# Half of one more part of a mixing stage moved between the experts, with its sums kept in DRAM

## The chip, the cores and the metric

The kernel runs on one core of a Trainium2 chip. The metric is the device time of one execution in microseconds (us). Engines are named as the profile names them: PE (matrix multiplication; PEld is its weight load), DVE (elementwise work, scans and reductions), ACT (activation functions), POOL (elementwise work, no access to PSUM), SP (issues the DMAs).

## The reference, cut to what matters

Two layers run over x of 16 batches, 256 tokens and 128 features, all in float32. Layer 0 is attention with 16 heads, then a mixture of 16 experts. Layer 1 is a "holographic" attention, then a token mixing block. The change concerns the passage from the experts to the holographic attention, whose core is (H = 16 heads of 64, so 1024 columns; T = 256):

```python
h = _layernorm(x) * (1 + ca) + sa
k = exp(1j * (h @ Wk) * 10)            # a phase for each token and column
v = h @ Wv
rotors = exp(1j * t * freqs)           # the same for all batches
out_pos   = real(cumsum(v * rotors)          * conj(rotors)) / sqrt(t + 1)
out_assoc = real(cumsum(v * conj(shifted k)) * k)            / sqrt(t + 1)
out = (out_pos * gate[:, 0] + out_assoc * gate[:, 1]) @ Wo
x = x + ga * out
```

The real part of a product of complex numbers is two real sums (cosine and sine), so each column needs four running sums over time: two for `pos` (the rotor's half) and two for `assoc`.

## The kernel before

Two batches make a chunk: eight chunks of 512 tokens (`NCH`). The 1024 columns of the holographic attention are eight parts of 128 (`NJ`), numbered 0 to 7. The kernel has three stages.

**Attention of layer 0** (0 to 304 us). The change doesn't touch it.

**Experts** (304 to 672 us). A loop over 128 steps, step n being expert e = n mod 16 of chunk c = n div 16. `gate_up(n)` multiplies the gate and the up weights into PSUM (pg, three banks, line 764; pup, two banks, line 766); DVE makes g (line 768), ACT u (770) and the Silu (773), POOL clamps u (774). One step later `act(n-1)` lets DVE make the product (780) and POOL weigh it by the score (781); three steps later `down(n-3)` adds it into the chunk's accumulator (789). The score rows come as `wide` loads on SP, four steps ahead. All the compute engines run in the order in which the program issues their instructions.

Between the steps stands other work, each piece at a fixed e, or a generator that advances once a step:
- e = 2 to 4: the end of the chunk before (`chunk_end1`, `with_tokens`, `into_stream`). e = 5: DVE takes mean and variance of its rows (`figures`, lines 182 and 183). e = 7: POOL makes the factors (`normalizer`, lines 188 to 193). These are "the stream's figures".
- `prepare` (as `ready`) makes rotors, scaled weights and, in `first_steps`, the first two parts of the late stage. `past_others` keeps its matmuls out of steps in which others use the one spare PSUM bank `p_m`.
- `last_end` finishes the last chunk's attention and its routing (steps 1 to some 34).
- `part_ahead(c)` (line 885) starts at e = 8 of the next chunk, for the six chunks below `AHEAD`. It computes part 7 of chunk c in full, in eight pieces (pos or assoc, batch k, cosine or sine s) of 256 elements: POOL multiplies (`bind`, 903), a step later DVE scans (909) and multiplies by gate and probe (911), a step later DVE adds (916). A piece takes two steps. The sum stays in SBUF in `totals[c]`.

**Holographic attention and mixing** (673 to 1060 us, then an end of 20). A loop over 58 steps (c, j): 7 parts in each of the first six chunks, 8 in the last two. In step n PE projects keys and values of step n+2 (pk 1135, pv 1139), ACT rounds (`whole`, 1136) and copies v; DVE scans `assoc` (1172, into `m_assoc`), scans `pos` (into the PSUM tile `mem`), takes the phase of step n+2 (`phases`, off, 1151) and multiplies mem by the rotor (m_pos, 1408); POOL multiplies m_assoc of step n-1 by its phasor (1413) and binds both halves of step n+1 (1169); ACT makes the sines of step n+2 (1157 to 1159); PE multiplies m_assoc of n-1, later m_pos of n, into the chunk's output `pos[c]` (1186, two matmuls each). At j = 3 one matmul adds `totals[c]` with `w_last` (1195). At j = 0 ACT reads the output of the chunk before (`gated_out`, 1204). The mixing block of the chunks before is spread over the same steps by `place`; its figures come from running sums on ACT (`mix_means`, `mix_figures`, lines 1242 and 1251) and two operations on POOL (`mix_spread`, 1266).

At the end the last two batches run as two generators, advanced together by `both_halves`, beside the last outputs of the chunk before (`mix_out`).

Of the kernel before, what the change touches and what calls it, by code (L numbers as in the profile page):

```python
# [41 lines left out]
AHEAD = NCH - 2  # L42
PARTS = [NJ - 1 if c < AHEAD else NJ for c in range(NCH)]
# [11 lines left out]
def tile_adaln_two_layers(ctx: ExitStack, tc: tile.TileContext, a: dict, out: bass.AP):  # L55
# [130 lines left out]
    def normalizer(c, mv, pool, tag):  # L186
# [7 lines left out]
        return rstd, off  # L194

# [31 lines left out]
    with ExitStack() as moe_scope:  # L227
# [500 lines left out]

        late = ctx.enter_context(tc.tile_pool(name="late", bufs=1, side="right"))
# [11 lines left out]
        w_last = load_late("w_last", [P, D], a["Wo"][HD - P :, :])  # L741
        w_assoc = load_late("w_assoc", [P, NJ, D], a["Wo"].rearrange("(j p) f -> p j f", p=P))
        with ExitStack() as scope:
# [141 lines left out]
            def part_ahead(c):  # L885
# [9 lines left out]
                v = cross.tile([P, 2, T], F32, tag="o", name=f"v_ahead_{c}")  # L895
                pv = p_m.tile([P, 2, T], F32, tag="m", name=f"pv0_{c}")
                nc.tensor.matmul(pv, w_v1[:, ts(j, P)], flat, start=True, stop=True)
                nc.scalar.copy(v, pv)
                bound = {}

                def bind(nm, k, s, by):
                    t = cross.tile([P, T], F32, tag=("heads", "y")[s], name=f"bound_ahead_{nm}_{c}_{k}_{s}")
                    nc.gpsimd.tensor_tensor(t, v[:, k, :], by, ALU.mult)
                    bound[nm, k, s] = t

                written = set()

                def read(nm, k, s, i, probe):
                    nc.vector.tensor_tensor_scan(row, keep_all, bound.pop((nm, k, s)), 0.0, ALU.mult, ALU.add)
                    dst = row if k in written else totals[c][:, k, :]  # L910
                    nc.vector.scalar_tensor_tensor(dst, row, gates[:, j, i : i + 1], probe, ALU.mult, ALU.mult)

                def added(k):
                    if k in written:
                        dst = totals[c][:, k, :]
                        nc.vector.tensor_tensor(dst, row, dst, ALU.add)
                    written.add(k)
# [3 lines left out]
                pos_ = [("pos", k, s, 0, rotor[:, j, s, :], rotor[:, j, s, :]) for k in range(2) for s in range(2)]  # L921
                assoc_ = [("assoc", k, s, 1, cs[:, s, k, 0:T], cs[:, s, k, 1:]) for k in range(2) for s in range(2)]
# [7 lines left out]
                pieces = assoc_ + pos_  # L930
# [6 lines left out]
                for i in range(9):  # L937
                    if i:
                        yield
                        q = pieces[i - 1]  # L940
                        read(*q[:4], q[5])
                    if i < 8:
                        q = pieces[i]
                        bind(*q[:3], q[4])
                    yield
                    if i:
                        added(pieces[i - 1][1])

            def past_others(steps=1):

                while any((at["step"] + i) % NE in (3, 7, *range(10, 16)) for i in range(steps)):
                    yield

            def first_steps():

                flat = hTs[0].rearrange("p k t -> p (k t)")
                for n in range(2):
# [68 lines left out]
            totals = [late.tile([P, 2, T], F32, tag=f"total{c}", name=f"total{c}") for c in range(AHEAD)]  # L1026
# [34 lines left out]
            for n in range(total + 4):  # L1061
# [21 lines left out]
                if e == 5 and c:  # L1083
                    mv = figures(c - 1, "a1")
                if e == 7 and c:
                    figs[c - 1] = normalizer(c - 1, mv, fp, "a1")
# [9 lines left out]
                if e == 8 and 1 <= c <= AHEAD:  # L1096
                    ahead.append(part_ahead(c - 1))
# [6 lines left out]
    with ExitStack() as scope:  # L1104
# [16 lines left out]
        another(hp1)  # L1121
# [38 lines left out]

        def rot(n):
            return rotor[:, steps[n][1], :, :].unsqueeze(2).to_broadcast(both)

        def binders(n):
            w = work[n]
            v2 = w["v"].unsqueeze(1).to_broadcast(both)
            for nm, bind in (("pos", rot(n)), ("assoc", phasor[n % 3][:, :, :, 0:T])):
# [3 lines left out]
        def summed(n, nm, dst):  # L1171
            nc.vector.tensor_tensor_scan(  # L1172
                dst.rearrange("p s k t -> p (s k t)"),
                keep.rearrange("p s t -> p (s t)"),
                work[n][nm].rearrange("p s k t -> p (s k t)"),
# [5 lines left out]
        def out_project(n, i, w, m):  # L1181
# [11 lines left out]
            if i == 0 and j == 3 and c < AHEAD:  # L1193

                nc.tensor.matmul(
                    pos[c], w_last, totals[c].rearrange("p k t -> p (k t)"), start=False, stop=False
                )
# [30 lines left out]
        mix = {}  # L1228

# [7 lines left out]

        def mix_means(c, pool=hp):
            total, less = (pool.tile([P, 4], F32, tag=f"{nm}_f1", name=f"{nm}_f1_{c}") for nm in ("total", "less"))
            unused = hp.tile([P, D], F32, tag="unused", name=f"unused_{c}", bufs=1)  # L1240
            for i in range(4):
                nc.scalar.activation(unused, x[2 * c + i // 2][:, i % 2, :], AF.Copy, accum_out=total[:, i : i + 1])
            nc.scalar.activation(less, total, AF.Copy, scale=-1.0 / D)
            mix[c] = unused, less

        def mix_figures(c, pool=hp):

            unused, less = mix[c]
# [130 lines left out]
        for n in range(last + 2):  # L1379
# [18 lines left out]
            if n <= last:  # L1398
# [4 lines left out]
                if n:  # L1403
                    summed(n, "assoc", m_assoc)
# [194 lines left out]
```

## Time and profile before

| | us |
|---|---|
| time before, median of 3 runs | 1081.39 (1079.85 to 1081.78) |
| the profiled execution's own time | 1081.84 |
| its span, first to last instruction | 1080.1 |
| first gate matmul of the experts | 303.4 |
| first scan of the late stage | 673.4 |
| a gate matmul to the next, in most expert steps | 2.57 |
| the same for 16 steps (64 to 80) | 45.5 |
| m_pos to m_pos, parts 3 to 6 of chunks 2 to 5 | 6.43 |
| seven late steps, chunks 2 to 4 | 46.9 |

Mean times of single operations, from the groups of instructions (line, shape, ns):

| operation | ns |
|---|---|
| DVE scan, 128x1024 (1172) | 2282 and 2274 |
| DVE scan, 128x256 (909) | 691 |
| DVE product m_pos, 128x1024 (1408) | 1215 |
| DVE product, gate and probe, 128x256 (911) | 484 to 493 |
| DVE add, 128x256 (916) | 418 |
| POOL product, 128x1024 (1169, 1413) | 2182 |
| POOL product, 128x256 (903) | 704 |
| POOL clamp and product, 128x512 (774, 781) | 634, 1281 |
| ACT sum of a row, 128x128 (1242) and its read | 306, 186 |
| ACT squares of a row, 128x128 (1251) and its read | 398, 187 |

How to read the profile: busy time of an engine is the sum of its records, which overlap a little at their ends; a float32 matmul is two MATMUL records. In the timeline a line has start, length, engine, source line, operation, output and inputs; in brackets stands the idle time of the engine before it and who ended it. In windows the columns are the busy times of PE, PEld, DVE, ACT and POOL, then the granted PE clock as a share of full speed, and the DMA's share.

### The profile page before, as it was taken

What the parts mean: (1) busy time and instruction counts of PE and PEld (TensorE: products, weight loads), DVE (VectorE), ACT (ScalarE), POOL (GpSimd) and SP (SyncE); (2) the same over time, 40 slices, a digit from 0 to 9 for tenths busy, and PEclk for the clock granted to TensorE, in tenths of its full rate; (3) what the DMA queues carried; (4) which work ended last, traced back from release to release, by engine and by line L of the source; (5) the groups of instructions that cost most, each with busy time, mean ns of one, the idle gap of its engine ahead of it and who ended that gap; (6) DMA issues with size and microseconds to landing.
All of it is one profiled execution on the core that took longest, in us unless ns stands there. A gap on an engine that the chain in (4) does not pass through costs nothing.

```text
span 1080.1 us, 16033 instructions
## 1 busy us (share of the span) xinstructions
PE 1023.5 (95%) x5333; PEld 519.6 (48%) x5333; DVE 909.9 (84%) x1409; ACT 682.3 (63%) x1383; POOL 803.1 (74%) x750
## 2 busy tenths in 40 slices
PE   7999999999999999999999999889999999999987
PEld 5566666666654444444444444333444343434434
DVE  6678878998756789887777778999999999999995
ACT  3676677667656566676766554556676666767662
POOL 2245434533557678888877888999999999999992
PEclk8999999999999999999999999999999999999999
DMA  4102100000052222222222221000000000000000
GB/s 116 42 11 61 53 13 3 2 4 2 4 175 95 82 99 85 93 99 99 95 82 88 89 98 59 1 0 0 1 5 6 10 1 10 1 10 5 5 11 20
DMA packets 31955, 46.80 MB, mean 43 GB/s; under 512 B 8032, under 2 KB 22784, under 8 KB 31872
## 3 DMA queue, kind: packets, MB, share of 16 engines
q1 hardware_dynamic: 31328, 45.51, 12.8%
q8 instruction: 42, 0.69, 0.3%
q14 instruction: 41, 0.34, 0.1%
q10 hardware_dynamic: 544, 0.26, 0.1%
HBM read 43.13 MB, written 2.37 MB: 42 GB/s over the span
## 4 chain that ended last, share of the span: by engine, by line
PE 59%; DVE 23%; ACT 6%; POOL 6%; issue 4%; DMA 1%; SPq 0%; DVEq 0%; ACTq 0%; POOLq 0%
PE pg L764 9%; PE acc L789 9%; PE pup L766 9%; DVE sum_assoc L1172 7%; DVE mem L1172 6%; PE s L404 5%; PE st L438 5%; PE po L458 5%; DVE m_pos L1408 4%; PE pout L1186 3%; PE pq L531 2%; DVE maxima L416 1%; POOL bound_pos L1169 1%; POOL u L781 1%; PE pk L539 1%
## 5 line engine op out<-in xcount | busy, mean ns | idle before, releaser
L446 ACT ACTIVATE exp<-st 128x512 f32<-128x512 f32 x256 | 132.2, 602 | 87.0 <-PE st L438 87.0
L416 DVE TENSOR_REDUCE maxima<-s 128x2 f32<-128x512 f32 x256 | 159.0, 685 | 26.5 <-PE s L404 26.3
L781 POOL TENSOR_TENSOR u<-u,wide 128x512 f32<-128x512 f32 x128 | 163.9, 1281 | 16.1 <-DVE u L780 6.3
L770 ACT ACTIVATE u<-pup,b_gu 128x512 f32<-128x512 f32 x128 | 87.6, 684 | 108.9 <-PE pup L766 100.9
L1186 PE MATMUL pout<-m_pos,w_pos 128*128 128x512 f32 x228 | 114.7, 627 | 32.1 <-DVE m_pos L1408 23.2
L768 DVE TENSOR_SCALAR g<-pg,b_gu 128x512 f32<-128x512 f32 x128 | 95.6, 747 | 58.2 <-PE pg L764 56.9
L789 PE MATMUL acc<-u,w_dn 128*128 128x512 f32 x256 | 132.3, 599 | 3.0 <-POOL u L781 2.8
L1172 DVE TENSOR_TENSOR_SCAN sum_assoc<-keep,bound_assoc 128x1024 f32<-128x1024 bf16 x58 | 132.3, 2282 | 1.8 <-POOL bound_assoc L1169 1.7
L1172 DVE TENSOR_TENSOR_SCAN mem<-keep,bound_pos 128x1024 f32<-128x1024 bf16 x58 | 131.9, 2274 | 0.0
L764 PE MATMUL pg<-hT,w_gu 128*128 128x512 f32 x256 | 131.5, 595 | 0.4 <-DVE logits L638 0.4
L766 PE MATMUL pup<-hT,w_gu 128*128 128x512 f32 x256 | 130.7, 592 | 0.0
L1169 POOL TENSOR_TENSOR bound_assoc<-v,phasor 128x1024 f32<-128x1024 f32 x57 | 124.3, 2181 | 3.9 <-ACT phasor L1159 3.9
L1413 POOL TENSOR_TENSOR sum_assoc<-sum_assoc,phasor 128x1024 f32<-128x1024 f32 x58 | 126.6, 2183 | 0.4 <-DVE sum_assoc L1172 0.4
L1169 POOL TENSOR_TENSOR bound_pos<-v,rotor 128x1024 f32<-128x1024 f32 x57 | 124.4, 2182 | 0.0
L774 POOL TENSOR_SCALAR u<-u 128x512 f32<-128x512 f32 x128 | 81.1, 634 | 56.6 <-ACT u L770 49.8
L1186 PE MATMUL pout<-sum_assoc,w_assoc 128*128 128x512 f32 x228 | 107.5, 594 | 1.2 <-POOL sum_assoc L1413 1.2
L780 DVE SCALAR_TENSOR_TENSOR u<-u,pg 128x512 f32<-128x512 f32 x128 | 87.0, 679 | 15.7 <-POOL u L774 14.4
L1186 PEld LDWEIGHTS pout<-m_pos,w_pos 128*128 128x128 f32 x228 | 40.4, 192 | 102.0 <-DVE m_pos L1408 53.5
L773 ACT ACTIVATE pg<-g 128x512 f32<-128x512 f32 x128 | 76.1, 594 | 16.8 <-DVE g L768 16.7
L1136 ACT ACTIVATE whole<-pk 128x512 f32<-128x512 f32 x56 | 33.4, 596 | 84.2 <-PE pk L1135 84.0
L438 PE MATMUL st<-qx,kx 32*128 32x256 f32 x1024 | 82.4, 390 | 0.9 <-DMA qx<-turned 0.8
L404 PE MATMUL s<-kx,qx 32*128 32x256 f32 x1024 | 78.1, 409 | 4.2 <-DVE kx L541 1.8
(305 smaller groups left out, 1835.1 us busy)
## 6 DMA issues: line engine op xcount, KB each, us to landing
wide<-scores SPq DMA_DIRECT2D x64, 512.0 KB
qx<-turned SPq DMA_DIRECT2D x256, 1.0 KB
w_gu<-in_gate_up_dram SPq DMA_DIRECT2D x8, 256.0 KB
out_dram<-x SPq DMA_DIRECT2D x16, 128.0 KB
x<-in_x_dram SPq DMA_DIRECT2D x14, 128.0 KB
w_dn<-in_down_dram SPq DMA_DIRECT2D x4, 256.0 KB
ga<-ga_rows SPq DMA_DIRECT2D x1, 768.0 KB
w_k<-in_Wk_dram SPq DMA_DIRECT2D x1, 512.0 KB
```

The costliest lines, as they stand in the source:

```text
L404: nc.tensor.matmul(s[g][:, i, :], qs[c][r][rows_, k, ts(i, P)], ks[c][rows_, r // NS, k, :], start=True, stop=True,)
L416: nc.vector.tensor_reduce(mx[:, :, g], s[g], AX.X, ALU.max, negate=True)
L438: nc.tensor.matmul(st[g][:, i, :], ks[c][rows_, r // NS, k, ts(i, P)], qs[c][r][rows_, k, :], start=True, stop=True,)
L446: nc.scalar.activation(e[:, g, :, :], st[g], AF.Exp, scale=QSCALE)
L764: nc.tensor.matmul(pg, w_gu[:, e, 0 : 2 * D : 2], h2, start=True, stop=True)
L766: nc.tensor.matmul(pu, w_gu[:, e, 1 : 2 * D : 2], h2, start=True, stop=True)
L781: nc.gpsimd.tensor_tensor(u, u, wide[n // SOME][:, n % SOME, :], ALU.mult)
L789: nc.tensor.matmul(accs[c], w_dn[:, e, :], work.pop(n), start=False, stop=(e == NE - 1))
L1169: nc.gpsimd.tensor_tensor(w[nm], v2, bind, ALU.mult)
L1172: nc.vector.tensor_tensor_scan(dst.rearrange("p s k t -> p (s k t)"), keep.rearrange("p s t -> p (s t)"), work[n][nm].rearrange("p s k t - ...
L1186: nc.tensor.matmul(pos[c], w[:, j, :], m[:, k, :, :].rearrange("p k t -> p (k t)"), start=(j == 0 and i == 0 and k == 0), stop=(c < NCH - ...
L1413: nc.gpsimd.tensor_tensor(m, m, phasor[(n - 1) % 3][:, :, :, 1:], ALU.mult)
```

## The change

- Among the experts, `part_ahead` becomes `parts_ahead`: it also computes the `pos` half of part 6, so there are twelve pieces instead of eight and one more values matmul for each of the six chunks (at e = 0). A piece is bound in steps with e mod 4 not 0, and read, product and add included, in the step after it. The twelve pieces end at e = 0, sixteen steps after the first.
- The sums of parts 6 and 7 are stored to DRAM (two DMAs of 256 KB for each chunk, on SP) and fetched in the late stage at j = 1 (`fetched`), to be multiplied at j = 6 and j = 3 (`with_fetched`). `w_last` holds two parts' weights.
- In the late stage, a step of part 6 in the first six chunks is a half step (`is_half`): no binding, scan or products of `pos`; the scan of `assoc` is cut in two (cosine into `mem`, sine into `m_assoc`); DVE multiplies the cosine half, POOL only the sine half; one matmul with the fetched sum stands where two with m_pos stood.
- The stream's figures among the experts (e = 5, 6, 7) are made by `mix_means`, `mix_figures` and `mix_spread` instead of `figures` and `normalizer`.
- All three phasor tiles are made in `first_steps`, and its matmuls keep out of e = 0 as well.
- At the end one `both_halves` goes ahead of the two `mix_out`.

```diff
-            def part_ahead(c):
+            def parts_ahead(c):
...
+                def read(q, nm, k, s, i, probe):
+                    nc.vector.tensor_tensor_scan(row, keep_all, bound.pop((q, nm, k, s)), 0.0, ALU.mult, ALU.add)
+                    dst = sum_of[q][:, k, :]
+                    more = (q, k) in written
+                    gate = gates[:, q, i : i + 1]
+                    nc.vector.scalar_tensor_tensor(row if more else dst, row, gate, probe, ALU.mult, ALU.mult)
+                    if more:
                         nc.vector.tensor_tensor(dst, row, dst, ALU.add)
...
+                yield
+                yield
+
+                vs[j - 1] = values(j - 1)
+                pieces = assoc + pos_ + pos_before
+                late_one = None
+                for step in range(1, NE + 1):
+                    yield
+                    if late_one:
+                        read(*late_one[:5], late_one[6])
+                        late_one = None
+                    if step % 4 and pieces:
+                        late_one = pieces.pop(0)
+                        bind(*late_one[:4], late_one[5])
+                for q in (j, j - 1):
+                    nc.sync.dma_start(totals[c, q], sum_of[q])
...
-                while any((at["step"] + i) % NE in (3, 7, *range(10, 16)) for i in range(steps)):
+                while any((at["step"] + i) % NE in (0, 3, 7, *range(10, 16)) for i in range(steps)):
...
                 if e == 5 and c:
-                    mv = figures(c - 1, "a1")
+                    mix_means(c - 1, fp, behind)
+                if e == 6 and c:
+                    mix_figures(c - 1, fp)
                 if e == 7 and c:
-                    figs[c - 1] = normalizer(c - 1, mv, fp, "a1")
+                    mix_spread(c - 1, fp)
+                    figs[c - 1] = mix.pop(c - 1)
...
-            for nm, bind in (("pos", rot(n)), ("assoc", phasor[n % 3][:, :, :, 0:T])):
+            for nm, bind in (("pos", rot(n)), ("assoc", phasor[n % 3][:, :, :, 0:T]))[is_half(n) :]:
...
+        def fetched(c):
+
+            for q in (NJ - 1, NJ - 2):
+                t = hp.tile([P, 2, T], F32, tag=f"there{q}", name=f"fetched_{c}_{q}", bufs=1)
+                nc.sync.dma_start(t, totals[c, q])
+                pos[c, q] = t
...
+                if half:
+
+                    summed(n, "assoc", mem, slice(0, 1))
+                    summed(n, "assoc", m_assoc, slice(1, 2))
+                elif n:
                     summed(n, "assoc", m_assoc)
-                summed(n, "pos", mem)
+                if not half:
+                    summed(n, "pos", mem)
                 if n and n + 2 <= last:
                     phases(n + 2)
-                nc.vector.tensor_tensor(m_pos, mem, rot(n), ALU.mult)
+                if half:
+                    nc.vector.tensor_tensor(m_assoc[:, 0], mem[:, 0], phasor[n % 3][:, 0, :, 1:], ALU.mult)
+                else:
+                    nc.vector.tensor_tensor(m_pos, mem, rot(n), ALU.mult)
...
-                nc.gpsimd.tensor_tensor(m, m, phasor[(n - 1) % 3][:, :, :, 1:], ALU.mult)
+                part = slice(1 if is_half(n - 1) else 0, 2)
+                nc.gpsimd.tensor_tensor(m[:, part], m[:, part], phasor[(n - 1) % 3][:, part, :, 1:], ALU.mult)
...
-                out_project(n, 0, w_pos, m_pos)
+                if is_half(n):
+                    with_fetched(c, j, w_last[:, 0])
+                else:
+                    out_project(n, 0, w_pos, m_pos)
+                if j == 1 and c < AHEAD:
+                    fetched(c)
+                if j == 3 and c < AHEAD:
+                    with_fetched(c, NJ - 1, w_last[:, 1])
...
         both_halves()
+        both_halves()
         for k in range(2):
             mix_out(2 * gone + k, py[:, k])
-        both_halves()
         both_halves()
```

## The prediction

> **What bounds the kernel now.** I read the page first, then the windows by stage, then the timeline of two places that the change touches.
>
> ```profile
> PE 1023.5 (95%) x5333; PEld 519.6 (48%) x5333; DVE 909.9 (84%) x1409; ACT 682.3 (63%) x1383; POOL 803.1 (74%) x750
> ...
> PE 59%; DVE 23%; ACT 6%; POOL 6%; issue 4%; DMA 1%; SPq 0%; DVEq 0%; ACTq 0%; POOLq 0%
> ```
>
> The averages mix two stages with different bounds, which the windows separate (columns: length, then PE, PEld, DVE, ACT and POOL busy).
>
> ```profile
> 487.00:533.00 46.00, 46.00 (x116) 20.90 (x116) 35.26 (x67) 33.85 (x70) 37.88 (x48) 1.00 0.26 93
> ...
> 880.00:930.00 50.00, 46.93 (x117) 20.40 (x116) 48.45 (x39) 35.76 (x76) 48.94 (x25) 1.00 0.02 6
> ```
>
> The reader is to see where the busy time reaches the window's length: among the experts (304 to 672) PE does, in the late stage (673 to 1060) DVE and POOL are at 97%. Costs on the path are counted from start to start in the timeline, since records overlap: a matmul of 512 columns is two PE records of 0.59 that start 0.43 apart, 0.86 in all, and an expert step of three takes 2.57; a late step takes 6.43. So the change carries work from a stage bound by DVE to one bound by PE. All times below are us.
>
> **The half step.** Part six in a chunk of the before, c=2 (step n=20), and the next scan:
>
> ```profile
> 805.51 1.21 DVE L1408 TENSOR_TENSOR m_pos<-mem,rotor 128x1024 f32<-128x1024 f32 x1
> ...
> 806.64 0.41 DVE L1303 TENSOR_TENSOR x<-py,x 128x256 f32<-128x256 f32 x1
> ...
> 806.77 1.99 PE L1186 MATMUL pout<-m_pos,w_pos 128*128 128x512 f32 x4 [0.57 <-DVE m_pos L1408]
> 806.97 2.28 DVE L1172 TENSOR_TENSOR_SCAN sum_assoc<-keep,bound_assoc 128x1024 f32<-128x1024 bf16 x1
> ...
> 808.60 0.60 PE L212 MATMUL pln_f<-ident,hn_f 128*128 128x128 f32 x4
> ...
> 809.03 1.02 PE L1135 MATMUL pk<-hT,w_k 128*128 128x512 f32 x2
> ...
> 809.17 2.27 DVE L1172 TENSOR_TENSOR_SCAN mem<-keep,bound_pos 128x1024 f32<-128x1024 bf16 x1
> ...
> 810.09 0.60 ACT L1136 ACTIVATE whole<-pk 128x512 f32<-128x512 f32 x1 [1.44 <-PE pk L1135]
> ...
> 811.35 0.67 DVE L1151 SCALAR_TENSOR_TENSOR off<-whole,pk 128x512 f32<-128x512 f32 x1
> ...
> 811.94 1.21 DVE L1408 TENSOR_TENSOR m_pos<-mem,rotor 128x1024 f32<-128x1024 f32 x1
> ...
> 813.40 2.28 DVE L1172 TENSOR_TENSOR_SCAN sum_assoc<-keep,bound_assoc 128x1024 f32<-128x1024 bf16 x1
> ```
>
> The reader is to see a second chain beside DVE's: m_pos of step 19 ends, PE starts its products (806.77), transposes, makes pk, ACT rounds it (whole, done 810.69), and DVE's `off` needs that. Today `off` comes 0.66 later than it must.
>
> On paper the half step takes from DVE a scan (2.20 start to start) and about half of m_pos (1.13 to 0.60, from a line through 256 elements at 0.41 and 1024 at 1.21): 2.7. From POOL it takes 2.13 + 1.07, from PE 0.86. But PE's chain is untouched. The two half scans end near 809.3 (each about 1.22, between the 0.69 of 256 elements and the 2.28 of 1024), `off` still can't start before 810.72, so DVE stands 1.4. Then 0.59 for `off`, 0.60 for the half product, 0.33 for x: the next scan at 812.25 instead of 813.40, a gain of **1.15**. The scans' price doesn't enter; the product could lie between 0.33 and 1.13, so 0.6 to 1.4. Chunks 2 to 5: 4.6. In chunk 1 (no x) the same walk (whole done 764.43, `off` today 764.75) gives 0.8. In chunk 0 the next scan waits 1.48 for POOL's bound_assoc at 719.88; POOL saves 2.13, and that scan starts 2.1 earlier. **Sum −7.5**. It is kept: `off` of the first step of the next chunk feeds cosines, oT, then PE's pos, and all shift together. PE rests there longer, 1.7 instead of 1.03.
>
> Row, then rule: after PE's idle of 3.84 before 727.86 the granted clock was 0.60 in the window from 729 to 732, and four matmul records took 3.68 instead of 1.98; after an idle of 1.91 before 1053.25 the four took 1.98. The Trainium skill ("TensorE: Matmul & The Clock Gate", Part 1) halves the clock after an idle window of about 3.4 us; by it 1.7 is harmless, and were it not, four chunks would lose an estimated 1.7 each.
>
> **The experts' stage.** Per chunk it gains:
> - PE: one `values` matmul at e=0, 0.86, on the path. Six: +5.15. In chunk 2, PE's gate matmuls start 0.9 late in steps 32 to 35 behind DVE's routing; some 0.5 of its matmul falls into that. +4.6.
> - DVE: four more pieces (scan 0.73, gated product 0.41 or 0.53, add 0.34: 1.14 without and 1.60 with the add), and two more adds; minus the moved statistics (414.30 to 415.91, 1.6). A step with a read is 0.67 + 0.60 + 1.60 = 2.87 on DVE against PE's 2.57, three in four; the fourth gives 1.3 back. The lag peaks at 1.6 at e=4 (x adds 0.66). A gate bank (there are three) is wanted again 2.74 after its last reader in most steps (start of pg of step n+3 less the end of the u of line 780 of step n, from the timeline), so the lag hides. Without this cover each step over it pays 0.3. In chunk 2 the slack is 0.06 to 1.7, but the first read moves from step 32 to 34 and the statistics go; walked through, no stall is left.
> - POOL: four more binds (0.67 each start to start), minus two small operations of `normalizer` (0.44). A step's clamp and product take 0.55 + 1.20 start to start (0.63 and 1.28 in the groups), so four steps hold 4 × 1.75 + 3 × 0.67 = 9.0 of 10.3: hidden, and without that cover 0.67 for each bind.
> - ACT: sums and squares by rows of the late stage, four at 0.43 + 0.20 and four at 0.52 + 0.21: 1.9 at e=5, 2.3 at e=6, and one copy 0.58. ACT idles 1.4 in a step, so it lags 1 to 2; the products' slack before `down` (start of acc less the end of line 781's u) is 2.15 in most steps. In chunk 4 the rotors' sines (0.4 to 0.9 in each step) make it 2.6: +0.7.
> - The first steps' pk moves from e=1 to e=4, behind the x that frees its bank: +0.5 (a matmul placed so waits 0.48 at 547.97).
> - In chunk 1 PE waits 0.75 at 378.88 for a product behind `normalizer` and DVE: −0.8.
>
> Row, then rule against: "ScalarE: Activation LUTs" (What ACT_TABLE_LOAD costs) prices each switch of set at about 2.66, and squares between Silus could cost two per chunk, an estimated 37 in seven. The trace's last load is at 402.17 (1.28), and Silu, sine and the late squares all run after it; I take none.
>
> Stores and fetches, 256 KB each: SP waits for the last read at e=0, and behind it is the `wide` load of e=2, not due for ten us. The fetch has from part 1 to part 3, 14 us; the last output, 128 KB, lands some 3.5 after its source. Hidden.
>
> **Stage +5.0.**
>
> **The seam.** The last piece moves behind the last expert's product:
>
> ```profile
> 671.90 0.69 DVE L780 SCALAR_TENSOR_TENSOR u<-u,pg 128x512 f32<-128x512 f32 x1 [0.66 <-POOL u L774]
> 671.94 2.49 POOL L781 TENSOR_TENSOR u<-u,wide 128x512 f32<-128x512 f32 x2
> 672.76 0.48 DVE L1117 MEMSET keep<- 128x512 f32 x1 [0.18 <-DVE u L780]
> ...
> 673.42 2.30 DVE L1172 TENSOR_TENSOR_SCAN mem<-keep,bound_pos 128x1024 f32<-128x1024 bf16 x1
> ```
>
> The reader is to see that DVE goes straight from the last u into the late stage, and stays busy to 691. Now a bind sits between the two products (PE's last matmuls +0.5), DVE reads the piece of step 126's bind before the last u (to 673.0), waits for the last bind (673.65), reads 1.60, then the memset: the first scan at 675.95, **+2.5**. POOL's 0.5 would be the least, 3.5 the most if PE's clock stays halved longer there.
>
> **The end.** One `both_halves` goes ahead of two outputs: r no longer waits behind 0.66 of x, but the last x now do: −0.35 (0 to −0.66).
>
> **Sum:** 5.0 + 2.5 − 7.5 − 0.35 = −0.4. The profiled execution took 1081.84 (span 1080.1), 0.45 above the median of 1081.39; on the median: **1081.0**.
>
> **Rivals.**
> 1. *Slower: DVE's reads become PE's wait among the experts.* It decides where the lag (1.6, plus what sines, routing or POOL add) passes the slack of a gate bank. For: slack is 0.06 to 1.7 in steps 32 to 38, and DVE hardly rests from 394 to 434. Against: 2.74 nearly everywhere else. Price: one lost group of three read steps, 0.9, in each of six chunks: +5.4, 1086.4. Chance 0.28 (with a halved clock).
> 2. *Faster: the half step gives what it saves.* If whole is ready earlier than I walked, six times 2.7 = 16, 1072; against it, the program's order puts pk behind m_pos. More likely is a part: the seam costs POOL's 0.5 only, or PE's six matmuls find more idle time (stalls of 1.1 in chunk 2, 0.4 in chunk 3): 1078. Chance 0.30 together.
> 3. *It doesn't do what it says*: a fetch comes late and PE stands at part 3. Inside rival 1's chance, 0.03.
>
> My forecast, within 0.2% (2.2 us, about what a measurement of this kernel can tell): 0.42, its own range 1079.2 to 1083.2. For 8 in 10 the range takes the probable part of rival 2 and nearly all of rival 1: 1077.0 to 1086.0.
>
> **What would show it.** DVE idle about 1.4 before `off` in the half steps, released by whole: right; none: rival 2. Chunk periods among the experts up 0.86: right; up over 1.5 with PE released by DVE or POOL: rival 1. First scan of the late stage 2.5 after the point where it stood, measured from the last gate matmul. Wrong altogether if PE halves its clock in the late stage, if a table load stands at each square, or if PE waits for a DMA.

## The result, and the profile after

The changed kernel is slower: 1087.41 us median of 6 runs against 1081.59 of 6 runs of the kernel before on the same chip, ratio 1.0063, 95% interval 1.0043 to 1.0084. The forecast was 1081.0. Its profiled execution took 1086.98, span 1085.2; the page's first lines (busy times, then the chain of waits by engine):

```profile
PE 1023.4 (94%) x5333; PEld 519.3 (48%) x5333; DVE 915.4 (84%) x1413; ACT 710.0 (65%) x1515; POOL 798.9 (74%) x754
...
PE 51%; DVE 23%; POOL 10%; ACT 8%; issue 6%; DMA 1%; SPq 0%; DVEq 0%; ACTq 0%; POOLq 0%
```

PE's busy time is what it was; DVE is busy 6 us more and ACT 28 (the sums and squares). POOL's share of the chain went from 6% to 10% and ACT's from 6% to 8%, though POOL is busy 4 us less. So what POOL adds to the chain is not longer work; something now waits for it. The windows of the two stages, same places as before:

```profile
487.00:533.00 46.00, 45.20 (x114) 20.15 (x113) 37.59 (x65) 36.08 (x86) 38.06 (x48) 1.00 0.31 104
880.00:930.00 50.00, 46.95 (x117) 20.56 (x116) 47.02 (x42) 34.78 (x74) 47.43 (x25) 1.00 0.06 16
```

Among the experts no engine besides PE comes near the 46 us, and PE itself fell from 46.00 to 45.20. Averages hide what follows, so I cut the span at three events: the **stage** from the first to the last gate matmul of the experts, the **seam** from there to the first 1024-element scan of the late stage, and the **late** part to the end.

| | first gate matmul at | stage | seam | late | span |
|---|---|---|---|---|---|
| before | 303.41 | 365.09 | 4.92 | 406.68 | 1080.1 |
| after | 301.11 | 375.99 | 8.92 | 399.18 | 1085.2 |
| difference | -2.3 | +10.9 | +4.0 | -7.5 | +5.1 |

The first column is scatter: in the kernels derived from the changed one, whose code up to there is the same, it runs from 300.94 to 305.30. The stage is firm: two kernels with the same code there differ by 0.13 at most (pairs below). The late part is less firm: in the eight kernels below that share its code with the changed one it runs from 398.36 to 401.33. Within that it paid back what was forecast, and the experts and the seam cost 14.9 instead of 7.5.

**Where the 10.9 lies.** From the starts of the gate matmuls, step by step, after less before: 0.84 to 0.87 at e=0 of chunks 2, 3, 4, 5 and 7, which is the `values` matmul; 1.57 at e=4 of chunk 6 (that chunk's matmul, 0.86, put the first steps' pk off to here, where it waits 0.7); less 0.7 absorbed in chunks 1 and 2. That is 5.1, as forecast. The other 5.8 are stalls that stood in no term: at e=10 of chunks 2, 3, 4 and 6 (0.98, 0.49, 1.06, 0.47), and in chunk 7 mostly at steps 121 and 122 (0.59, 1.40).

The groups show what DVE does there (busy, mean ns | idle just before, and what ended it). Two lines are the scans of the pieces, the third is `down`; first the kernel before, then the changed one:

```profile
L909 DVE TENSOR_TENSOR_SCAN sums<-sums,bound_ahead_pos 128x256 f32<-128x256 f32 x24 | 16.6, 692 | 0.0
L909 DVE TENSOR_TENSOR_SCAN sums<-sums,und_ahead_assoc 128x256 f32<-128x256 f32 x24 | 16.6, 690 | 0.0
...
L789 PE MATMUL acc<-u,w_dn 128*128 128x512 f32 x256 | 132.3, 599 | 3.0 <-POOL u L781 2.8
```

```profile
L960 DVE TENSOR_TENSOR_SCAN sums<-sums,und_ahead_pos 128x256 f32<-128x256 f32 x48 | 33.4, 695 | 21.8 <-POOL und_ahead_pos L956 21.6
L960 DVE TENSOR_TENSOR_SCAN sums<-sums,d_ahead_assoc 128x256 f32<-128x256 f32 x24 | 16.7, 694 | 6.0 <-POOL d_ahead_assoc L956 6.0
...
L833 PE MATMUL acc<-u,w_dn 128*128 128x512 f32 x256 | 133.0, 601 | 7.7 <-POOL u L825 7.7
```

DVE stood idle 27.8 in front of these scans, 27.6 of it until the bind on POOL was done; in the kernel before that idle time is 0.0 in both groups. The wait for POOL's product in front of `down` went from 2.8 to 7.7, and ACT's wait for g in front of the Silu from 16.7 to 41.8. The timeline of all engines at e=6 to e=8 of chunk 2:

```profile
416.03 0.40 ACT L213 ACTIVATE unused<-x,less_f 128x128 f32<-128x128 f32 x1
...
417.47 0.67 ACT L814 ACTIVATE u<-pup,b_gu 128x512 f32<-128x512 f32 x1
...
418.22 0.61 POOL L818 TENSOR_SCALAR u<-u 128x512 f32<-128x512 f32 x1 [1.52 <-ACT u L814]
...
420.15 1.02 POOL L228 TENSOR_TENSOR rstd_f<-off_f,neg_half 128x4 f32<-128x4 f32 x1
...
421.41 0.73 POOL L956 TENSOR_TENSOR und_ahead_pos<-v_ahead,rotor 128x256 f32<-128x256 f32 x1
...
422.17 0.70 DVE L960 TENSOR_TENSOR_SCAN sums<-sums,und_ahead_pos 128x256 f32<-128x256 f32 x1 [2.50 <-POOL und_ahead_pos L956]
...
423.77 0.74 DVE L812 TENSOR_SCALAR g<-pg,b_gu 128x512 f32<-128x512 f32 x1
...
424.24 1.12 PE L833 MATMUL acc<-u,w_dn 128*128 128x512 f32 x2 [0.71 <-POOL u L825]
...
424.55 0.60 ACT L817 ACTIVATE pg<-g 128x512 f32<-128x512 f32 x1 [0.84 <-DVE g L812]
```

The reader is to see a ring. ACT's squares put its u off; POOL's clamp waits 1.52 for that u; behind the clamp stand a product, the power of 1.02 and the bind; DVE waits 2.50 for the bind, and behind that scan in DVE's order stands g of the next expert; ACT's Silu waits for this g. Now ACT, POOL and DVE are all late, and PE waits for the product.

Why was the scan not late before? In a quiet place of the kernel before:

```profile
491.93 0.64 POOL L903 TENSOR_TENSOR und_ahead_assoc<-v_ahead,phasor_ahead 128x256 f32<-128x256 f32 x1
...
494.73 0.69 DVE L909 TENSOR_TENSOR_SCAN sums<-sums,und_ahead_assoc 128x256 f32<-128x256 f32 x1
```

The scan comes 2.16 after the bind has ended. After the change, a bind at 490.20 (0.64 long) and its scan at 490.87 lie 0.03 apart, and DVE has already stood idle 0.18 for it. In the old code the generator yields twice between a bind and its read, so two steps lie between them in program order (the text ahead of the prediction says "a step later", which is the distance in time only: POOL runs about a step behind DVE). The new loop yields once, and POOL's lag takes up all of it.

### The profile page after: what moved, and what is told of

Same layout as the page of the kernel before. It is cut to its first block, busy times and chain, and to the rows that moved or that the text cites. A ratio compares the mean times of both kernels' runs of the same rounds, so it can differ in the third digit from the quotient of the medians.

```text
span 1085.2 us, 16254 instructions
## 1 busy us (share of the span) xinstructions
PE 1023.4 (94%) x5333; PEld 519.3 (48%) x5333; DVE 915.4 (84%) x1413; ACT 710.0 (65%) x1515; POOL 798.9 (74%) x754
## 4 chain that ended last, share of the span: by engine, by line
PE 51%; DVE 23%; POOL 10%; ACT 8%; issue 6%; DMA 1%; SPq 0%; DVEq 0%; ACTq 0%; POOLq 0%
DVE sum_assoc L1236 6%; DVE mem L1236 6%; PE pg L808 6%; PE acc L833 5%; PE s L440 5%; PE pup L810 5%; PE st L474 5%; PE po L494 5%; PE pout L1250 4%; POOL u L825 3%; DVE m_pos L1455 3%; PE pq L567 2%; PE pk L1195 2%; ACT unused L204 2%; DVE maxima L452 1%
## 5 line engine op out<-in xcount | busy, mean ns | idle before, releaser
L1250 PE MATMUL pout<-m_pos,w_pos 128*128 128x512 f32 x204 | 103.1, 629 | 33.5 <-DVE m_pos L1455 22.3
L1236 DVE TENSOR_TENSOR_SCAN sum_assoc<-keep,bound_assoc 128x1024 f32<-128x1024 bf16 (+1 forms) x58 | 125.7, 2168 | 0.2 <-POOL bound_assoc L1233 0.2
L1461 POOL TENSOR_TENSOR sum_assoc<-sum_assoc,phasor 128x1024 f32<-128x1024 f32 (+1 forms) x58 | 121.2, 2090 | 1.5 <-DVE sum_assoc L1236 1.3
L1236 DVE TENSOR_TENSOR_SCAN mem<-keep,bound_pos 128x1024 f32<-128x1024 bf16 x52 | 118.2, 2273 | 0.0
L1233 POOL TENSOR_TENSOR bound_pos<-v,rotor 128x1024 f32<-128x1024 f32 x51 | 111.3, 2183 | 2.3 <-ACT v L1200 2.3
L817 ACT ACTIVATE pg<-g 128x512 f32<-128x512 f32 x128 | 76.2, 596 | 42.1 <-DVE g L812 41.8
L833 PEld LDWEIGHTS acc<-u,w_dn 128*128 128x128 f32 x256 | 46.7, 189 | 75.0 <-issue 41.5
L1250 PEld LDWEIGHTS pout<-m_pos,w_pos 128*128 128x128 f32 x204 | 36.6, 194 | 95.9 <-DVE m_pos L1455 47.7
```

The lines of the kernel that those rows point to most:

```text
L833: nc.tensor.matmul(accs[c], w_dn[:, e, :], work.pop(n), start=False, stop=(e == NE - 1))
L1233: nc.gpsimd.tensor_tensor(w[nm], v2, bind, ALU.mult)
L1236: nc.vector.tensor_tensor_scan(dst[:, half].rearrange("p s k t -> p (s k t)"), keep.rearrange("p (s k) t -> p s k t", k=2)[:, half].rearra ...
L1250: nc.tensor.matmul(pos[c], w[:, j, :], m[:, k, :, :].rearrange("p k t -> p (k t)"), start=(j == 0 and i == 0 and k == 0), stop=(c < NCH - ...
L1461: nc.gpsimd.tensor_tensor(m[:, part], m[:, part], phasor[(n - 1) % 3][:, part, :, 1:], ALU.mult)
```

## The experiments

All of them are edits of the changed kernel unless said otherwise. Medians, ratios to runs of the kernel before on the same chip, with 95% intervals, and the three lengths of the profiled execution (which, with its start as scattered as above, can lie up to 4 us off the median):

| kernel | median | ratio | stage | seam | late |
|---|---|---|---|---|---|
| figures_dve | 1085.64 | 1.0043 (1.0026 to 1.0059) | 373.94 | 8.88 | 398.90 |
| two_steps | 1082.88 | 1.0018 (1.0005 to 1.0031) | 371.73 | 7.66 | 400.14 |
| both | 1083.98 | 1.0016 (1.0002 to 1.0031) | 371.52 | 7.65 | 398.36 |
| eight_pieces | 1081.66 | 1.0001 (0.9989 to 1.0012) | 373.79 | 4.98 | 399.65 |
| before_sums | 1083.91 | 1.0020 (1.0009 to 1.0032) | 367.21 | 5.04 | 407.51 |
| two_early | 1086.55 | 1.0049 (1.0037 to 1.0061) | 374.53 | 6.32 | 401.33 |
| one_step_moved | 1086.76 | 1.0055 (1.0037 to 1.0074) | 376.08 | 7.53 | 400.54 |
| early_not_seven | 1082.91 | 1.0017 (1.0004 to 1.0029) | 372.57 | 6.31 | 399.34 |
| two_early_dve | 1089.86 | 1.0075 (1.0059 to 1.0091) | 377.98 | 6.31 | 399.25 |
| before_keys | 1080.04 | 0.9997 (0.9985 to 1.0010) | 365.06 | 4.93 | 406.55 |
| keys_first | 1076.95 | 0.9961 (0.9946 to 0.9976) | 371.86 | 7.65 | 393.79 |
| early_keys | 1079.99 | 0.9986 (0.9977 to 0.9995) | 374.49 | 6.32 | 394.91 |
| one_step_keys | 1079.68 | 0.9994 (0.9981 to 1.0006) | 376.09 | 7.53 | 392.34 |
| early_not_seven_keys | 1076.74 | 0.9961 (0.9947 to 0.9975) | 372.60 | 6.31 | 393.79 |

My theory (A) was that the one step between bind and scan closes the ring when ACT is late. The rivals: (B) ACT's sums alone, (C) twelve pieces are too much work.

### Sums, spacing, number of pieces

figures_dve puts the stream's figures back:

```diff
-                    mix_means(c - 1, fp, behind)
-                if e == 6 and c:
-                    mix_figures(c - 1, fp)
+                    mv = figures(c - 1, "a1")
                 if e == 7 and c:
-                    mix_spread(c - 1, fp)
-                    figs[c - 1] = mix.pop(c - 1)
+                    figs[c - 1] = normalizer(c - 1, mv, fp, "a1")
```

> The kernel after, with the stream's figures back on DVE and POOL as in the kernel before. Theory A (a read of DVE stands one step behind its bind on POOL, and POOL stands behind ACT, which is late by the sums at e=5 and e=6): without the sums POOL comes in time, the stalls of PE's gate matmuls at e=10 in chunks 2, 3, 4 and 6 (0.98, 0.49, 1.06, 0.47 in the kernel after) go, those near the end (0.59 and 1.40 at steps 121 and 122) in part; stage from first to last gate matmul 376.4 less 3 to 4.5, time 1083 to 1084.5. Theory B (ACT's sums alone make PE late): the stage loses all of the 5.6 of stalls, time 1082. Theory C (twelve pieces are simply too much for DVE and POOL): DVE gets 1.6 more per chunk, so the stalls grow; 1088 to 1092.

Short of A, and none of the three as it stands: the stage lost 2.05 (A wanted 3 to 4.5, B all 5.6), and the time of 1085.64 lies above A's. The stalls at e=10 of chunks 2, 4 and 6 went entirely, as A and B have it; chunk 3's grew (0.55, 1.10 and 0.28 at e=9 to 11), as C has it, and 1.37 at step 122 stayed. DVE's idle time before the scans is still 20.6 (16.8 and 3.8).

two_steps:

```diff
-                for step in range(1, NE + 1):
-                    yield
-                    if late_one:
-                        read(*late_one[:5], late_one[6])
-                        late_one = None
-                    if step % 4 and pieces:
-                        late_one = pieces.pop(0)
-                        bind(*late_one[:4], late_one[5])
+                bound_at = {}
+                for step in range(0, NE + 1):
+                    if step:
+                        yield
+                    if step - 2 in bound_at:
+                        q = bound_at.pop(step - 2)
+                        read(*q[:5], q[6])
+                    if step % 4 != 3 and pieces:
+                        q = bound_at[step] = pieces.pop(0)
+                        bind(*q[:4], q[5])
```

> The kernel after, each bind one step earlier, so that two steps lie between a bind and its read; the reads stay where they are. Theory A: DVE's waits for the bind (2.50 at 422.17, 1.71 at 663.65, 0.46 to 0.82 elsewhere) go, g and the product come in time though ACT's sums stay; the stage loses 4 to 5.6, time 1082 to 1083.5. Theory B: ACT is as late as it was, so POOL's product and acc are too; the stage changes by less than 1.5, time 1086 to 1087.5. Theory C: the same work in the same steps, no more than 1 gained, 1086.5 to 1087.5.

As A has it. The stage lost 4.3 of the 5.8, the seam 1.3. Its groups, same three lines as above:

```profile
L960 DVE TENSOR_TENSOR_SCAN sums<-sums,und_ahead_pos 128x256 f32<-128x256 f32 x48 | 33.1, 689 | 0.0
L960 DVE TENSOR_TENSOR_SCAN sums<-sums,d_ahead_assoc 128x256 f32<-128x256 f32 x24 | 16.5, 689 | 0.0
...
L833 PE MATMUL acc<-u,w_dn 128*128 128x512 f32 x256 | 133.9, 605 | 4.6 <-POOL u L825 4.4
```

The 27.8 of waits are gone. This kernel also has no bind at e=7, where the one with one step has one; the two are taken apart further down. What is left of stalls stands at e=10 of chunks 2 and 4 (0.4 each) and in chunk 7.

both is figures_dve and two_steps together.

> The figures back on DVE and each bind one step earlier. Theory A: no stall is left for DVE to pass on, but its load rises by 1.6 in a chunk and uses up the gate banks' slack in places; stage 371 to 373, time 1081.5 to 1084. Theory B: like figures_dve, 1082. Theory C: DVE carries all of the added work, 1088 to 1092.

Stage as in two_steps: with two steps between and these reads, it hardly matters where the figures are made. The stalls of chunks 2 and 4 went and 1.05 came in chunk 3.

eight_pieces:

```diff
-                pieces = assoc + pos_ + pos_before
+                pieces = assoc + pos_
...
-                    nc.sync.dma_start(totals[c, q], sum_of[q])
+                    nc.sync.dma_start(totals[c, q], sum_of[j])
```

> The kernel after without the four pieces that sum the rotor's half of part six (its binds, scans, products and adds are left out, part seven's total is stored in its place); the values matmul, its copy, the stores, the fetches, ACT's sums and the spacing of one step stay. Eight pieces stand at e=2 to e=12. Theory A: the e=6 to e=8 reads still stand behind late binds, so the stalls at e=10 (3.0 in the four chunks) stay; those after step 112 (about 2.1) go and the seam falls back from 8.5 to about 5; time 1081 to 1083. Theory B: the same as A. Theory C: the stalls go nearly all, stage 371, seam 4.5 to 5, time 1077.5 to 1079.

The stalls at e=10 of chunks 2, 4 and 6 are the same to 0.01 with eight pieces as with twelve (0.98, 1.05, 0.47), so C is out there; chunk 3's fell from 0.77 to 0.49, and chunk 7 lost most of its own. The seam is back at 4.98: its 4.0 belong to the four pieces. This does not part A from B, and leaving out the four pieces gives back nearly the whole loss (2.2 of the stage, 3.9 of the seam); that they need not cost it all is what two_steps shows.

### The sums alone, and where binds and reads stand

before_sums makes the mirror edit of figures_dve in the kernel before; nothing else of the change is in it.

> The kernel before with one part of the change alone: the stream's figures among the experts by running sums on ACT instead of DVE; eight pieces, each read two steps behind its bind. Theory A (it takes the sums and the read one step behind its bind together): the lateness of ACT and POOL at e=6 to e=8 is met by the second step and by the product's slack of 2.15 before down; at most a few tenths per chunk at e=10, less what DVE's relief gives; stage 365.1 minus 0.5 to plus 1, time 1080.5 to 1082. Theory B (the sums alone): the 3.0 of stalls at e=10 stand here too, 1084.

A missed here. The sums alone cost the stage 2.1: at e=9 to 11 of chunk 2 1.1, of chunk 4 0.4, of chunk 6 1.1, less some tenths in chunks 1 and 3. DVE's scans don't wait here (0.0), but POOL's clamp waits for ACT's u all the same (1.53 at 420.56), and the power follows. So the sums are a cost of their own, and B holds in part.

two_early (reads at e=1 to 3, 5 to 7, 9 to 11, 13 to 15; binds two steps ahead) starts the run of pieces one step earlier:

```diff
                 yield
-                yield
-
-                vs[j - 1] = values(j - 1)
...
+                    if step == 1:
+                        vs[j - 1] = values(j - 1)
```

> The kernel after, each bind two steps ahead of its read as in two_steps, and the whole run of pieces one step earlier than that: the reads stand at e=1 to e=15 (none at e=4, 8, 12), so the last read is done in step 127 and no piece lies behind the last expert's product. Theory A with the seam's part: the stage stays near two_steps' 371.7 (371 to 372), the seam, 7.66 there and 4.92 before, falls to 5 to 5.8; time 1080.3 to 1081.3. Rival: the seam is set by PE's last matmuls and POOL's last products, not by where the last read stands; seam 7 or more, time 1082.5 to 1083.

A surprise: no wait of DVE for a bind (0.0 in both groups), yet the stage is 374.53 where 371 to 372 was expected, and 3.5 of stalls stand at e=10 and 11. one_step_moved has two_steps' binds with two_early's reads, so one step between (`step - 1` for `step - 2` in two_steps):

> The kernel after with its twelve binds in the very steps of two_steps (e=0, 1, 2, 4, 5, 6, 8, 9, 10, 12, 13, 14: none at e=7, where POOL has the power of 1.02), but each read one step behind its bind as in the kernel after (none at e=4, 8, 12). Two_steps had both edits at once. Theory S (the spacing counts): DVE waits for the binds again and PE's gate matmuls stall at e=10 and at steps 121 and 122 as in the kernel after; stage 374.5 to 376. Theory P (what counts is where the bind stands on POOL, away from the power and from ACT's lateness): stage as in two_steps, 371 to 372.5. The last read is done one step earlier than in two_steps in either case, so the seam is 6 to 7; time 1080.5 to 1082 by P, 1084 to 1086 by S.

Theory S: DVE's idle time before the scans is back (21.7), the stage is 376.08 (the seam, 7.53, missed its 6 to 7). Taking the bind away from e=7 gains nothing as long as one step lies between. So spacing is needed, and, by two_early, is not enough. Left between two_steps and two_early were the reads' places and the bind at e=7. early_not_seven moves that bind alone (against two_early):

```diff
-                    if step - 2 in bound_at:
-                        q = bound_at.pop(step - 2)
+                    if step in bound_at:
+                        q = bound_at.pop(step)
...
-                    if step % 4 != 3 and pieces:
-                        q = bound_at[step] = pieces.pop(0)
+                    if step in (0, 1, 2, 4, 5, 6, 7, 9, 10, 12, 13, 14):
+                        q = bound_at[step + (3 if step == 7 else 2)] = pieces.pop(0)
```

> two_early with one bind moved: the one at e=7, where POOL has the power of 1.02, is issued at e=6; all reads stay (e=1 to 3, 5 to 7, 9 to 11, 13 to 15). Two_early's stage was 374.5 against 371.7 in two_steps, which has no bind at e=7 but reads at e=2 to 4, 6 to 8, 10 to 12. Theory P (the bind at e=7 holds up POOL's clamp while POOL is late): stage 371.5 to 372.7, seam 6.3, time 1083 to 1084. Theory R (the reads' place counts: a read of 1.6 at e=9, in the step in which DVE has to follow late products): stage 374 to 375, time 1086 to 1087.

Theory P: 2.0 of the stage for one bind of 0.64, six times. In two_early it stood on POOL behind the power, when POOL was already late: at e=7 of chunks 2, 3, 4 and 6 the clamp starts 3.9 to 4.8 after its gate matmul, against 2.75 in quiet steps. It put off the next clamp, which without it starts 0.6 sooner after its gate matmul in each of these chunks. early_not_seven and one_step_moved have the same reads and no bind at e=7, and differ by the binds' distance: 3.5. That confirms the spacing a second time.

two_early_dve is two_early with figures_dve's edit.

> two_early with the figures back on DVE, none of ACT's sums. If the stalls at e=10 come from ACT's sums, wherever reads and binds stand: those of chunks 2, 4 and 6 (0.78 and 0.49, 0.97, 0.38 in two_early) go; chunk 3's may grow by up to 1 as in figures_dve; stage 371.5 to 373.5, time 1083 to 1085. If DVE's reads or POOL's bind at e=7 make them without ACT: stage 374.5 or more, time 1086 to 1088.

The first guess is wrong and the second too low: the stage grew by 3.5, so stalls come without ACT's sums. The stalls of chunk 3 became 2.5 and those of chunk 6 1.1. With reads at e=5, 6 and 7 DVE has the statistics (1.6) and three pieces in a row, which would explain it; no run takes that apart. The figures are free on neither engine; which is dearer depends on the reads' steps.

### The half step

The prediction held that the half step is bound by ACT's whole. keys_first is two_steps with the keys of two steps later ahead of m_pos's products in the step before a half step:

```diff
-            keys()
-            values()
+            if n not in work:
+                keys()
+            if not keys_only:
+                values()
...
+            if n + 3 <= last and is_half(n + 1):
+                projected(n + 3, True)
             if n < last:
                 if is_half(n):
```

> two_steps with one edit in the late stage: the step ahead of a half step issues the key matmul and ACT's whole for two steps later ahead of the products of m_pos, not behind them. If the half step is held by whole, as the prediction walked it (DVE idle 1.43 before off at 820.51, done by ACT's whole), the wait goes, and the half step is then held by POOL's bound_assoc, which is done 1.3 before the scan that reads it; 1.0 to 1.3 in each of five half steps, some less in chunk 0: late stage 399 to 400 down to 393 to 395, time 1076.5 to 1078.5. Rival: POOL, 97% busy, takes the whole gain back in the next steps; late stage 398 to 400, time 1082 to 1083.

Late stage 393.79, from 400.14. Chunk 2's half step in the changed kernel, then in keys_first:

```profile
817.88 1.20 DVE L1236 TENSOR_TENSOR_SCAN sum_assoc<-keep,bound_assoc 128x512 f32<-128x512 bf16 x1
...
820.51 0.69 DVE L1211 SCALAR_TENSOR_TENSOR off<-whole,pk 128x512 f32<-128x512 f32 x1 [1.43 <-ACT whole L1196]
821.11 0.68 DVE L1453 TENSOR_TENSOR sum_assoc<-mem,phasor 128x512 f32<-128x512 f32 x1
...
822.04 2.28 DVE L1236 TENSOR_TENSOR_SCAN sum_assoc<-keep,bound_assoc 128x1024 f32<-128x1024 bf16 x1
```

```profile
811.89 1.02 PE L1194 MATMUL pk<-hT,w_k 128*128 128x512 f32 x2
...
813.95 1.19 DVE L1240 TENSOR_TENSOR_SCAN sum_assoc<-keep,bound_assoc 128x512 f32<-128x512 bf16 x1
...
815.06 0.66 DVE L1215 SCALAR_TENSOR_TENSOR off<-whole,pk 128x512 f32<-128x512 f32 x1
...
816.79 2.29 DVE L1240 TENSOR_TENSOR_SCAN sum_assoc<-keep,bound_assoc 128x1024 f32<-128x1024 bf16 x1
```

The idle 1.43 before `off` is gone, because pk (811.89) no longer stands behind the products. From the first half scan to the next step's scan the changed kernel and two_steps take 5.11 to 5.30 in chunks 1 to 5, keys_first 3.96 to 4.00. Chunk 0's is 5.65 in two_steps and in keys_first (4.95 in the changed kernel); there DVE waits for POOL's bound_assoc, 0.89 and then 2.13.

before_keys makes the edit in the kernel before, ahead of part six.

> The kernel before with the late stage's edit of keys_first alone, in the step before each part six. If the edit pays only because a half step leaves DVE waiting for whole: DVE is the bound there without half steps, off already comes 0.66 later than it must, and nothing is gained; late stage 405.5 to 407.5, time 1080 to 1082. Rival: whole and POOL's phasor are late in ordinary steps too; late stage 402 to 404, time 1076 to 1079.

Nothing: it pays only where a half step leaves DVE waiting. early_keys and one_step_keys join it to two_early and one_step_moved, early_not_seven_keys to early_not_seven:

> two_early and keys_first together. If the parts add: stage 371 to 372, seam 5 to 5.8, late stage 393 to 395, time 1074.5 to 1076.5. If POOL takes the half step's gain back, as the rival of keys_first has it: 1080.3 to 1081.3.

> one_step_moved with the late stage's edit of keys_first (key matmul and whole ahead of the products of m_pos in the step before a half step), which took the late stage to 393.8. Theory P: stage 371 to 372.5, seam 6 to 7, late stage 393.5 to 395; time 1074.5 to 1076.5. Theory S: 1078 to 1080.

> early_not_seven with the late stage's edit of keys_first (late stage 393.8). Theory P: stage 371.5 to 372.7, seam 6.3, late stage 393 to 395, time 1075 to 1077, at or just below keys_first's 1076.95. Theory R: 1078.5 to 1080.

The lengths add: each has its own pattern's stage and seam and a late stage of 392.3 to 394.9. early_keys missed its 1074.5 to 1076.5 by the stage and the seam that two_early had missed. keys_first and early_not_seven_keys beat both kernels, by 0.4% against the kernel before, and don't differ from each other (1076.95, 1076.74).

## Why the prediction was wrong

**The step that failed** is in the experts' stage: "so the lag hides" for DVE, "hidden" for POOL, and ACT's lag of "1 to 2" set against a slack of 2.15, each engine by itself. The sums of work were right (12 of 16 steps, 2.87 and 1.30; the windows show no engine full). What was not priced is the wait that the change adds: DVE's read on POOL's bind, now one step away instead of two. With that wait the slacks are one and the same slack: a gate bank is wanted 0.5 after its last reader at e=8 of chunks 2, 3, 4 and 6, where 2.74 was counted on, and the product of e=7 comes so late that `down` stands for it (0.71 at 424.24, shown above). Size: 4.3 in the stage and 1.3 in the seam by two_steps (3.5 in the stage where the reads are the same and no bind stands at e=7). Of the 1.5 of stalls that remain there, some is ACT's sums (2.1 when alone); I did not take it further apart.

The slack of 2.15 was mis-read as well. It holds in most steps, but not where the sums fall. In the kernel before, the product of e=7 in chunk 2, and the first matmul of `down` that reads it:

```profile
423.77 1.27 POOL L781 TENSOR_TENSOR u<-u,wide 128x512 f32<-128x512 f32 x1
...
425.52 1.02 PE L789 MATMUL acc<-u,w_dn 128*128 128x512 f32 x2
```

From its end (425.04) to 425.52 lie 0.48; in chunks 3, 4, 5 and 6 the same slack is 0.12, 1.28, 0.90 and 0.07. An ACT that lags 1 to 2 at e=5 and e=6 is past most of these, and `down` then waits at e=10: before_sums has that stall in chunks 2, 4 and 6.

By its other steps:
- *Six `values` matmuls*, 5.15 less 0.5 absorbed: 0.84 to 0.87 each, right. *pk of the first steps* 0.5: 0.7. *Chunk 1* -0.8: -0.2. *Chunk 4's ACT lag* 0.7: 1.06 at e=10 there, 0.4 by the sums alone (before_sums); but chunk 2 stalls as long (0.98, and 1.1 by the sums alone), where none was foreseen.
- *Seam* 2.5: the walk was right for reads that don't wait; two_steps has 2.7. The changed kernel has 4.0, since DVE waits again:

```profile
678.75 0.70 DVE L960 TENSOR_TENSOR_SCAN sums<-sums,und_ahead_pos 128x256 f32<-128x256 f32 x1 [0.76 <-POOL und_ahead_pos L956]
...
680.35 0.74 DVE L812 TENSOR_SCALAR g<-pg,b_gu 128x512 f32<-128x512 f32 x1
...
684.12 0.70 DVE L960 TENSOR_TENSOR_SCAN sums<-sums,und_ahead_pos 128x256 f32<-128x256 f32 x1 [0.71 <-POOL und_ahead_pos L956]
```

  g of the last expert (680.35) stands behind the read of 678.75, though its gate matmul began at 677.10. Ending the pieces a step earlier (two_early) gave 6.3, not the expected 5 to 5.8; what holds the other 1.4 I did not try.
- *Half steps* -7.5: right, with its reason. 6.43 became 5.30 in chunks 2 to 5 (1.13; expected 1.15), 6.09 became 5.11 in chunk 1 and 7.66 became 4.95 in chunk 0 (5.65 in two_steps). DVE idles 1.43 before `off` behind whole, half scans take 1.2 and the half product 0.68. *End* -0.35: from the last scan to the end 24.8 became 24.7.
- *Rival 1* had the direction and nearly the size (1086.4) at a chance of 0.28, and what was to show it came (10.9 in six chunks, with PE released by POOL), but the mechanism was another: not that DVE falls behind by its own work, but that it stands behind POOL. The nearness of the size is luck.
- *Rival 2* thought 2.7 per half step out of reach because "the program's order puts pk behind m_pos". That order was the limit, and could be changed: in keys_first the half steps of chunks 2 to 5 take 3.97 instead of the 6.43 of before, a gain of 2.46.
- *The fetch* is never waited for, and *PE's longer rests* in the half steps cost no clock: from 690 to 1040 the granted clock is 0.99 before and after.
- *Table loads.* The trace after has the same four loads of 1.28 as before, and the 28 sums and 28 squares between the Silus add none. The Trainium skill ("ScalarE: Activation LUTs", What ACT_TABLE_LOAD costs) charges only a switch to a different set, and its figure for the load itself, about 1283 ns, is the trace's 1.28; by the trace neither the sums nor the squares cause a switch.

## What to carry to other kernels

When a change packs more pieces between the steps of a loop, count how many steps lie between a producer and its consumer on another in-order engine, before and after: a wait that was free at two steps cost at one here, because all that stands behind the consumer inherits the producer's lateness. Read a slack at the step where the new work falls, not where it is usual. Slacks of several engines must not be counted singly when their instructions wait for each other in a ring. Where shorter work on one engine leaves it waiting, look whether the other chain's first instruction stands behind something that can wait.

## What the runs showed of the hardware

The same DVE operation among the experts, `theta`, which reads two tiles in SBUF, took 0.69 or up to 1.26, and the short operations on POOL beside it grew in the other's turn. In two_steps:

```profile
424.07 1.27 POOL L825 TENSOR_TENSOR u<-u,wide 128x512 f32<-128x512 f32 x1
424.62 1.26 DVE L891 SCALAR_TENSOR_TENSOR theta<-turns,theta 128x512 f32<-128x512 f32 x1
425.30 1.09 POOL L956 TENSOR_TENSOR und_ahead_pos<-v_ahead,rotor 128x256 f32<-128x256 f32 x1
```

`theta` ends 0.54 after POOL's product does (425.34), and the bind, 0.63 to 0.74 in most places, ends 0.51 after `theta`. In the changed kernel, at 441.79, `theta` came first and took 0.69, and the clamp begun at 441.88 took 1.06 instead of 0.61. DVE's product of u with pg, which lies in PSUM, overlaps POOL's operations at 0.68. This agrees with the Trainium skill ("SBUF — State Buffer", SBUF: two separate sides): a DVE operation with two inputs in SBUF and a POOL operation that reads SBUF contend for ports that they share, and whichever starts first holds them for the whole instruction. And POOL's power of 128x4 elements takes 1.02, five times its product of that size (0.20): a small tile, but not a small operation.
